# LSTM with residual on one core: the first PSUM banks begin without the bias, x and Wx load first, and step 4's plain products move into the first h Wh

## The chip, the cores and the metric

The kernel runs on one core of one Trainium2 chip. The metric is the device time of one execution in microseconds; the median of several runs is compared. A core has TensorE (PE) for matmuls, which write to eight PSUM banks of 128 x 512 float32, VectorE (DVE), ScalarE (ACT), GpSimd (POOL), and SyncE (SP), which here issues the transfers. All arithmetic is float32.

## The reference

An LSTM over 512 steps for a batch of 32, input and hidden size 512, with a residual:

```
xW = x @ Wx + b                        # x (32, 512, 512), Wx (512, 2048)
for t in range(512):
    a = xW[:, t] + h @ Wh              # Wh (512, 2048), h starts as cond_1024, c as 0
    i, f, o = sigmoid(a[:, :512]), sigmoid(a[:, 512:1024]), sigmoid(a[:, 1024:1536])
    g = tanh(a[:, 1536:])
    c = f * c + i * g
    h = o * tanh(c)
    out[:, t] = x[:, t] + h
```

Only `h @ Wh` and what follows it depend on the step before. `x @ Wx` does not, and the kernel works it out ahead.

## The kernel before

One step's gates fill one PSUM bank of 128 x 512: the four column groups j of 32 partitions hold the batch of 32 for a quarter of the hidden units, and the free dimension holds four gates of 128. `h_part(t)` (L459) adds `h @ Wh` into it: for each of four row blocks k of Wh, four matmuls (one for each j) of 128 x 512. The profile counts each float32 matmul as two records, so a step has 32 of them. `cell(t)` (L472) applies sigmoid and tanh on ScalarE (L476 to L478), the products on VectorE (fc, ig, c, h at L485 to L493) and the transpose into `ht` (L495), which is the next step's stationary operand.

`x @ Wx` is done in two ways. From step 8 on (quads of four steps from `FIRST` = 2) it uses a fast matrix product of seven sub-products at two levels: sums of x blocks (`early_sums`, `late_sums`) and sums of weight blocks (`outer_weight` at L212, `inner_weight` at L217) are made on VectorE, multiplied in `inner` (L335) into the banks pa, pb and pp, and gathered by `first_add`, `second_add` and `seed` (L292 to L311). Steps 0 to 7 and the last eight use plain products instead: `direct(t, pairs)` (L355) adds the product of step t's x with pieces of Wx; a pair (k, gg) is one quarter of Wx, with two pieces e, and costs eight matmuls. Four pairs are the whole product of a step.

The banks of the steps are `ge` (even steps), `go[0]` (steps 1, 5, ...) and `go[1]` (steps 3, 7, ...). `clear(bank)` (L246) writes zeros with a matmul, after which products accumulate onto what is there. The bias gets into a step by being copied into the bank before the products (`set_bias`, on ScalarE, L379), or, at the very start, by the VectorE copies of L586. Step 2 has no bank of its own at the start; its products are made in step 3's bank, copied by ScalarE to SBUF (`park`, L387), and brought back later by `set_bias`.

The order on each engine is that in which the program is written (`tc.manual_schedule()`, L580). The main loop goes over k from 8 on, and k is called an iteration here: iteration k runs `h_part(k - 11)` if there is one, then the evacuations of the fast product (`evacuate`), bias copies, x sums, weight sums (`make_weights`, from the table `weights` at L515), the plain products of the start (`first_direct`, L544), the fast product's matmuls (`input_part`), the plain products of the table `direct_at`, and the cell. Iterations 8 to 10 have no step yet; iteration 11 has step 0.

Loads at the start (L194 to L208): half of x's chunk 0, two quarters of Wx, chunk 1 of x, two more quarters of Wx, four pieces of Wh and the other half of chunk 0 are issued by SP; the four bias pieces, each broadcast to 32 partitions, and h0 by ScalarE's queue. Transfers share eight semaphores in turn, so an issue may have to wait until the transfer eight places earlier has landed. In the trace x chunks are `xc`, the quarters of Wx `w`, the pieces of Wh `wh_sb`.

`start_sums` (L259) prepares db, a difference of bias parts, and the running sums xr1 and xr5 from the bias. In VectorE's order it stands between the first two weight sums and the first outer one.

Of the kernel before, what the change touches and what calls it, by code (L numbers as in the profile page):

```python
# [7 lines left out]
F32 = mybir.dt.float32  # L8
# [3 lines left out]
P = 128  # L12
# [16 lines left out]
def kernel(  # L29
# [38 lines left out]
    nc = tc.nc  # L68
# [4 lines left out]
    upool = ctx.enter_context(tc.tile_pool(name="upool", bufs=1))  # L73
# [9 lines left out]
    pp = psum.tile([P, 4, P], F32, name="pp")  # L83
    ge = psum.tile([P, G, P], F32, name="ge")
    go = [psum.tile([P, G, P], F32, name=f"go_{i}") for i in range(2)]
# [3 lines left out]
    def gates_of(t):  # L89
        if t >= 4 * LAST:  # L90
            return last_banks[t - 4 * LAST]
        return ge if t % 2 == 0 else go[(t % 4) // 2]
# [80 lines left out]
    def load_first(half):  # L173
        n = TC // 2
        nc.sync.dma_start(
            out=xcs[0][:, half * n : (half + 1) * n].rearrange("p t q b -> p (t q b)"),
            in_=x[0][:, half * n * P : (half + 1) * n * P],
        )

    bias_sb = const.tile([P, G, P], F32, name="bias_sb")  # L180
    h_init = const.tile([P, NJ, B], F32, name="h_init")
# [5 lines left out]
    def load_raw(k, gg):  # L187
        for e in range(2):
            nc.sync.dma_start(
                out=raw[k, gg][:, 2 * e : 2 * e + 2].rearrange("p s j u -> p (s j u)"),  # L190
                in_=wx[2 * k + gg][:, 2 * e * NJ * P : 2 * (e + 1) * NJ * P],
            )

    load_first(0)  # L194
    for j in range(NJ):
        nc.scalar.dma_start(
            out=bias_sb[j * B : (j + 1) * B, :, :],
            in_=bias[j].unsqueeze(0).to_broadcast([B, G, P]),
        )
    nc.scalar.dma_start(out=h_init.rearrange("p q b -> p (q b)"), in_=h0)  # L200
    load_raw(0, 0)
    load_raw(0, 1)
    load_chunk(1)
    load_raw(1, 0)
    load_raw(1, 1)
    for k in range(NJ):
        nc.sync.dma_start(out=wh_sb[:, k], in_=wh[:, k])
    load_first(1)  # L208

    def outer_weight(r):  # L210
        a, b = {5: (w12, w_sb[1]), 7: (w_sb[3], w12), 6: (w_sb[3], w_sb[5]), 4: (w_sb[2], w_sb[6])}[r]
# [143 lines left out]
    def direct(t, pairs, bank=None):  # L355

        c, tt = divmod(t, TC)
        bank = gates_of(t) if bank is None else bank
        fresh = not written(bank)
        for k, gg in pairs:  # L360
            for e in range(2):
                for j in range(NJ):
                    nc.tensor.matmul(  # L363
                        bank[j * B : (j + 1) * B, 2 * gg : 2 * gg + 2],
                        xcs[c][:, tt, 2 * k + e],
                        raw_blocks(k, gg, e, t >= 4 * LAST)[:, :, j],
                        start=fresh and (k, gg, e) == (0, 0, 0),
                        stop=True,
                        skip_group_check=True,
                    )  # L370

    def written(bank):

        return bank in (ge, *go, pp)

    parked = {}

    def set_bias(t):
        nc.scalar.copy(gates_of(t), parked.pop(t, bias_sb))  # L379

    def add_bias(t):
        nc.vector.tensor_add(gates_of(t), gates_of(t), bias_sb)

    def park(t, bank):

        parked[t] = upool.tile([P, 4, P], F32, name="parked", tag="u3")
        nc.scalar.copy(parked[t], bank)  # L387

    def quad_at(r, k, stage):

# [3 lines left out]
    def evacuate(k):  # L394

        for r in (1, 5, 6, 7):
            q = quad_at(r, k, 4)
            if q is not None:
                read_out(r, q)
        for q, rest in (divmod(k - 7, 4),):  # L400
            if rest == 0 and FIRST <= q < LAST:
                nc.vector.tensor_add(U[23, q][:, 1], U[7, q], U["p5", q])
        for q, rest in (divmod(k - 10, 4),):
            if rest == 0 and FIRST <= q < LAST:
                nc.vector.tensor_add(U["p5", q], U[4, q], U["p5", q])  # L405
        for q, rest in (divmod(k - 12, 4),):
            if rest == 0 and FIRST <= q < LAST:
                p5 = U["p5", q]
                nc.scalar.copy(ge[:, 2:4], p5[:, 0:2])
                nc.scalar.copy(go[1][:, 2:4], p5[:, 2:4])  # L410
        q = quad_at(2, k, 1)
        if q is not None:
            first_add23(q)
        for r in (5, 1, 4, 6, 7):
            q = quad_at(r, k, 1)
            if q is not None:
                first_add(r, q)
        q = quad_at(2, k, 2)
        if q is not None:
            second_add23(q)  # L420
        for r in (6, 7, 5, 4, 1):
            q = quad_at(r, k, 2)
            if q is not None:
                second_add(r, q)
        q = quad_at(2, k, 3)
        if q is not None:
            seed23(q)
        for r in (4, 6, 7, 5, 1):
            q = quad_at(r, k, 3)
            if q is not None:  # L430
                seed(r, q)
# [27 lines left out]
    def h_part(t):  # L459
        g = gates_of(t)  # L460
        for k in range(NJ):
            for j in range(NJ):
                nc.tensor.matmul(  # L463
                    g[j * B : (j + 1) * B],
                    state["ht"][:, k, :],
                    wh_sb[:, k, j, :],
                    start=False,
                    stop=True,
                    skip_group_check=True,
                )  # L470

    def cell(t):  # L472
# [44 lines left out]
        0: [(1, 7), (5, 6)],  # L517
        1: [(1, 4), (5, 7), 6, (6, 5)],
        2: [(5, 4), (6, 6)],
        3: [(6, 7), (2, 5), (3, 5)],  # L520
        4: [4, (6, 4)],
        5: [7, (7, 5)],
        6: [(7, 6), (2, 6), (3, 6), (4, 5)],
        7: [(7, 7), (2, 7), (3, 7)],
        8: [(7, 4), (4, 6)],
        9: [(3, 4)],
        10: [(2, 4), (4, 7)],
# [6 lines left out]
    def make_weights(k):  # L534
        for what in weights.get(k - 4 * FIRST, ()):
            make(what)


    ALL = ((0, 0), (0, 1), (1, 0), (1, 1))
    bias_at = {12: (2,), 13: (5,), 14: (4,), 15: (7,), 16: (6,)}  # L540
    direct_at = {k: [(t, ALL) for t in bias_at[k] if t > 2] for k in bias_at}
    direct_at[11], direct_at[12] = [(3, ALL[2:3])], [(3, ALL[3:4])]

    def first_direct(k):  # L544

        pairs = {8: ALL[0:2], 9: ALL[2:3], 10: ALL[3:4]}.get(k, ())
        for pair in pairs:
            direct(2, (pair,), gates_of(3))
            if k == 10:
                park(2, gates_of(3))  # L550
                set_bias(3)
            for t in (0, 1):
                direct(t, (pair,))
        if k == 10:
            direct(3, ALL[0:2])

# [4 lines left out]
    for k in range(504, WINDOWS):  # L561
# [9 lines left out]
        while todo and free_at[todo[0][0] - end] <= k and room > 0:  # L571
            t = todo[0][0]
# [7 lines left out]
    with tc.manual_schedule():  # L580
        warm = work.tile([P, G, P], F32, name="warm", tag="s")
        nc.scalar.activation(warm[:, 0], zero, AF.Sigmoid)
        for bank in (go[1], ge, go[0], pp):
            clear(bank)
        for t in (3, 0):
            nc.vector.tensor_copy(gates_of(t), bias_sb)  # L586
        set_bias(1)
        for what in weights[-1][:2]:
            make(what)
        start_sums()  # L590
        make(weights[-1][2])
        for op in early_sums(nc.vector, 1):
            op()
        make(weights[-1][3])
        early, late = {}, {}
        for k in range(4 * FIRST, WINDOWS):
            t = k - LEAD
            c, rest = divmod(k + 5, TC)
            if rest == 0 and 2 <= c < NCHUNK:
                load_chunk(c)  # L600
            if k == 4 * LAST + 1:
                reload()
            if t >= 0:
                h_part(t)
            evacuate(k)
            for i in bias_at.get(k, ()):
                set_bias(i)
            for i in bias_after:
                if bias_after[i] == k:
                    add_bias(i)  # L610
            for first, sums_of, made, cut in ((-1, early_sums, early, 5), (3, late_sums, late, 3)):
                c, rest = divmod(k - first, TC)
                if (2 if sums_of is early_sums else 1) <= c < NCHUNK - 1 and rest in (0, 2):
                    if rest == 0:
                        made[c] = sums_of(nc.vector, c)
                    for op in made[c][:cut] if rest == 0 else made.pop(c)[cut:]:
                        op()
            make_weights(k)
            if t < 0:
                first_direct(k)  # L620
            input_part(k)
            if t >= 0:
                for what in direct_at.get(k, ()):
                    direct(*what)
                cell(t)
# [43 lines left out]
```

## Time and profile before

| | us |
|---|---|
| median of 3 runs (lowest to highest) | 3164.57 (3163.84 to 3165.09) |
| the profiled execution | 3164.18 |
| its span, first to last instruction | 3162.3 |
| TensorE busy in the span | 3148.0 |
| VectorE busy | 2234.3 |
| ScalarE busy | 1274.1 |
| first plain product starts | 9.33 |
| h Wh of step 0 starts, its last piece starts | 24.88, 28.84 |
| h Wh of steps 1, 2, 3, 4, 5 starts | 31.99, 37.87, 45.63, 54.04, 63.33 |

When the inputs landed in the profiled execution, worked out as issue plus time to landing: first half of x 3.9 us; bias pieces 3.7, 5.4, 7.4, 8.45; h0 8.6; Wx pieces 6.3, 8.2, 9.9, 11.2, then 13.6, 14.9, 17.6, 18.9; chunk 1 of x 12.35; Wh pieces 21.3, 23.8, 26.3, 28.8; second half of x 29.4.

Times are of one execution by the profiler; what lies outside the span is 1.9 us. Matmuls are pipelined and overlap in the records, so lengths of groups are best read from start to start. A row of the timeline gives start, duration, engine, line, operation, destination and sources, shape and count, and in brackets the idle time of the engine before it and what ended it.

### The profile page before, as it was taken

What the parts mean: (1) busy time and instruction counts of PE and PEld (TensorE: products, weight loads), DVE (VectorE), ACT (ScalarE), POOL (GpSimd) and SP (SyncE); (2) the same over time, 40 slices, a digit from 0 to 9 for tenths busy, and PEclk for the clock granted to TensorE, in tenths of its full rate; (3) what the DMA queues carried; (4) which work ended last, traced back from release to release, by engine and by line L of the source; (5) the groups of instructions that cost most, each with busy time, mean ns of one, the idle gap of its engine ahead of it and who ended that gap; (6) DMA issues with size and microseconds to landing.
All of it is one profiled execution on the core that took longest, in us unless ns stands there. A gap on an engine that the chain in (4) does not pass through costs nothing.

```text
span 3162.3 us, 149307 instructions
## 1 busy us (share of the span) xinstructions
PE 3148.0 (100%) x66048; PEld 1894.6 (60%) x66048; DVE 2234.3 (71%) x9242; ACT 1274.1 (40%) x4186; POOL 237.5 (8%) x515
## 2 busy tenths in 40 slices
PE   9999999999999999999999999999999999999999
PEld 5666666666666666666666666666666666666653
DVE  6777777777777777777777777777777777777763
ACT  2434444444444444444344444444444444443432
POOL 0000000000000000000000000000000000000000
PEclk9999999999999999999999999999999999999999
DMA  3000000000000000000000000000000000000010
GB/s 137 26 28 20 28 20 28 26 21 26 27 21 28 20 28 26 20 28 20 28 27 21 26 28 20 28 20 28 26 21 26 22 25 27 21 26 28 20 34 13
DMA packets 49370, 86.45 MB, mean 27 GB/s; under 512 B 5456, under 2 KB 38480, under 8 KB 48208
## 3 DMA queue, kind: packets, MB, share of 16 engines
q1 hardware_dynamic: 48384, 76.57, 7.4%
q8 instruction: 516, 8.45, 1.1%
q14 instruction: 134, 1.10, 0.1%
q10 hardware_dynamic: 336, 0.33, 0.0%
HBM read 43.32 MB, written 33.55 MB: 24 GB/s over the span
## 4 chain that ended last, share of the span: by engine, by line
PE 98%; DMA 1%; DVE 1%; ACT 0%; issue 0%; ACTq 0%; DVEq 0%
PE ge L463 27%; PE go L463 27%; PE pa L335 18%; PE pp L335 10%; PE pb L335 6%; PE ge L335 5%; PE go L335 3%; DMA wh_sb<-in_L_cond_Wh_dram 1%; PE go L363 0%; PE pa L463 0%; PE ge L363 0%; PE pa L363 0%; DMA xc<-in_x_dram 0%; DMA bias_sb<-in_L_cond_b_dram 0%; PE pp L463 0%; PE pb L463 0%
## 5 line engine op out<-in xcount | busy, mean ns | idle before, releaser
L463 PE MATMUL go<-wh_sb,ht 128*32 128x512 f32 x8128 | 918.7, 592 | 0.0
L463 PE MATMUL ge<-wh_sb,ht 128*32 128x512 f32 x8064 | 911.5, 592 | 0.7 <-DVE ht L495 0.5
L485 DVE TENSOR_TENSOR fc<-s,c 128x128 f32<-128x128 f32 x511 | 149.3, 292 | 569.1 <-ACT s L476 569.1
L463 PEld LDWEIGHTS go<-wh_sb,ht 128*32 128x32 f32 x8128 | 256.7, 110 | 458.0 <-issue 455.1
L463 PEld LDWEIGHTS ge<-wh_sb,ht 128*32 128x32 f32 x8064 | 256.9, 110 | 455.4 <-issue 415.7
L506 POOL TENSOR_TENSOR oc<-xc,ht 128x128 f32<-128x128 f32 x511 | 237.3, 464 | 2915.9 <-DVE ht L495 1466.4
L476 ACT ACTIVATE s<-ge 128x256 f32<-128x256 f32 x253 | 97.2, 384 | 833.8 <-PE ge L463 833.8
L335 PE MATMUL pa<-w,n 128*32 128x128 f32 x5952 | 299.1, 273 | 1.4 <-DVE xr L296 1.4
L491 ACT ACTIVATE ig<-c 128x64 f32<-128x64 f32 x1024 | 205.8, 248 | 220.9 <-DVE c L489 220.9
L476 ACT ACTIVATE s<-go 128x256 f32<-128x256 f32 x254 | 97.5, 384 | 441.7 <-PE go L463 441.7
L493 DVE TENSOR_TENSOR fc<-s,ig 128x64 f32<-128x64 f32 x1024 | 189.9, 226 | 96.7 <-ACT ig L491 96.7
L335 PEld LDWEIGHTS pa<-w,n 128*32 128x32 f32 x5952 | 180.7, 110 | 78.8 <-issue 39.1
L335 PEld LDWEIGHTS pa<-w,na 128*32 128x32 f32 x3968 | 124.1, 110 | 148.8 <-issue 110.8
L275 ACT COPY u<-pp 128x512 f32<-128x512 f32 x248 | 145.4, 586 | 142.0 <-PE pp L335 142.0
L335 PE MATMUL pp<-w,sa 128*32 128x128 f32 x3968 | 199.4, 273 | 0.0
L335 PE MATMUL pa<-w,na 128*32 128x128 f32 x3968 | 199.4, 273 | 0.0
L335 PE MATMUL pa<-w,nb 128*32 128x128 f32 x3968 | 199.4, 273 | 0.0
L495 DVE STREAM_TRANSPOSE ht<-fc 128x64 f32<-128x64 f32 x1024 | 190.6, 224 | 1.5 <-DVE fc L493 0.9
L487 DVE TENSOR_TENSOR ig<-s 128x64 f32<-128x64 f32 x1024 | 181.1, 219 | 0.0
L489 DVE TENSOR_TENSOR c<-fc,ig 128x64 f32<-128x64 f32 x1024 | 180.5, 217 | 0.0
L405 DVE TENSOR_TENSOR p<-u,p 128x512 f32<-128x512 f32 x124 | 86.0, 694 | 114.5 <-ACT u L275 114.5
L335 PEld LDWEIGHTS pa<-w,nb 128*32 128x32 f32 x3968 | 121.4, 110 | 74.1 <-issue 37.9
(138 smaller groups left out, 5278.8 us busy)
## 6 DMA issues: line engine op xcount, KB each, us to landing
out_dram<-oc SPq DMA_DIRECT2D x255, 128.0 KB, 1.8
xc<-in_x_dram SPq DMA_DIRECT2D x63, 512.0 KB, 3.8
w<-in_L_cond_Wx_dram SPq DMA_DIRECT2D x10, 512.0 KB, 6.8
wh_sb<-in_L_cond_Wh_dram SPq DMA_DIRECT2D x4, 1024.0 KB, 14.6
xc<-in_x_dram SPq DMA_DIRECT2D x2, 256.0 KB, 9.5
bias_sb<-in_L_cond_b_dram ACTq DMA_DIRECT2D x4, 64.0 KB, 5.0
h_init<-in_cond_dram ACTq DMA_DIRECT2D x1, 64.0 KB, 6.0
out_dram<-oc SPq DMA_DIRECT2D x1, 64.0 KB, 1.6
```

The source lines that it names most:

```text
L275: nc.scalar.copy(u, pp)
L335: nc.tensor.matmul(dst[j * B : (j + 1) * B], operand(r, s, quad), w_sb[r][:, place(r, s), j], start=start, stop=True, skip_group_check=True,)
L405: nc.vector.tensor_add(U["p5", q], U[4, q], U["p5", q])
L463: nc.tensor.matmul(g[j * B : (j + 1) * B], state["ht"][:, k, :], wh_sb[:, k, j, :], start=False, stop=True, skip_group_check=True,)
L476: nc.scalar.activation(s[:, 0:2, :], g[:, 0:2, :], AF.Sigmoid)
L485: nc.vector.tensor_mul(fc, s[:, 1, :], state["c"])
L487: nc.vector.tensor_mul(ig[:, u], s[:, 0, u], s[:, 3, u])
L489: nc.vector.tensor_add(c[:, u], fc[:, u], ig[:, u])
L491: nc.scalar.activation(tc_t[:, u], c[:, u], AF.Tanh)
L493: nc.vector.tensor_mul(h[:, u], s[:, 2, u], tc_t[:, u])
L495: nc.vector.transpose(ht[:, 2 * i : 2 * i + 2].rearrange("p q b -> p (q b)"), h[:, u])
L506: nc.gpsimd.tensor_add(state["oc"][:, tt % 2], xcs[n][:, tt], ht)
```

## The change

- Loads: both quarters of Wx for k = 0 go ahead of the bias; the bias and h0 are issued by SP too, h0 after the other quarters of Wx; the second half of x's chunk 0 goes between Wh pieces 1 and 2.
- Banks: `clear(go[1])`, the two bias copies of L586 and `set_bias(1)` at the start go. For steps below 4 outside pp the first product starts the bank afresh (`fresh`). The bias of steps 0, 1 and 2 is added by VectorE after their products: step 2's as it is parked (a sum from bank to SBUF in place of ScalarE's copy), steps 0 and 1 by `add_bias` in iteration 10, step 3 by `add_bias` in iteration 13.
- Step 4: its plain products (four pairs, 64 records) leave iteration 14. They are made in the bank pp, which ScalarE fills with the bias at the start, between the Wh pieces of step 0: two pairs ahead of piece 2 and two ahead of piece 3. ScalarE then copies pp to SBUF (`parking(4, "u2")`), and `set_bias(4)` brings it back in iteration 14.
- Weight sums (2,5) and (3,5) move from iteration 11 to 14, (4,5) from 14 to 15. `make_weights` comes after `first_direct`.

The resulting order on VectorE at the end of iteration 10 and in 11 is: evacuations, the parking sum, add_bias(0), add_bias(1), two weight sums (L217), second_add(5), the lower half of seed(1) into pp (L311), three x sums, one weight sum, cell 0.

```diff
     load_first(0)
+    load_raw(0, 0)
+    load_raw(0, 1)
     for j in range(NJ):
-        nc.scalar.dma_start(
+        nc.sync.dma_start(
             out=bias_sb[j * B : (j + 1) * B, :, :],
             in_=bias[j].unsqueeze(0).to_broadcast([B, G, P]),
         )
-    nc.scalar.dma_start(out=h_init.rearrange("p q b -> p (q b)"), in_=h0)
-    load_raw(0, 0)
-    load_raw(0, 1)
     load_chunk(1)
     load_raw(1, 0)
     load_raw(1, 1)
+    nc.sync.dma_start(out=h_init.rearrange("p q b -> p (q b)"), in_=h0)
     for k in range(NJ):
+        if k == 2:
+            load_first(1)
         nc.sync.dma_start(out=wh_sb[:, k], in_=wh[:, k])
-    load_first(1)
...
-        fresh = not written(bank)
+        fresh = t < 4 and bank is not pp or not written(bank)
...
-    def park(t, bank):
-
-        parked[t] = upool.tile([P, 4, P], F32, name="parked", tag="u3")
-        nc.scalar.copy(parked[t], bank)
+    def parking(t, tag):
+
+        parked[t] = upool.tile([P, 4, P], F32, name=f"parked_{t}", tag=tag)
+        return parked[t]
...
         for k in range(NJ):
+            if t == 0 and k >= 2:
+                direct(4, ALL[2 * k - 4 : 2 * k - 2], pp)
...
-        3: [(6, 7), (2, 5), (3, 5)],
+        3: [(6, 7)],
...
-        6: [(7, 6), (2, 6), (3, 6), (4, 5)],
-        7: [(7, 7), (2, 7), (3, 7)],
+        6: [(7, 6), (2, 5), (3, 5), (2, 6), (3, 6)],
+        7: [(7, 7), (2, 7), (3, 7), (4, 5)],
...
-    direct_at = {k: [(t, ALL) for t in bias_at[k] if t > 2] for k in bias_at}
+    direct_at = {k: [(t, ALL) for t in bias_at[k] if t not in (2, 4)] for k in bias_at}
...
             if k == 10:
-                park(2, gates_of(3))
-                set_bias(3)
+                nc.vector.tensor_add(parking(2, "u3"), gates_of(3), bias_sb)
             for t in (0, 1):
                 direct(t, (pair,))
+                if k == 10:
+                    add_bias(t)
...
-        for bank in (go[1], ge, go[0], pp):
+        for bank in (ge, go[0], pp):
             clear(bank)
-        for t in (3, 0):
-            nc.vector.tensor_copy(gates_of(t), bias_sb)
-        set_bias(1)
+        nc.scalar.copy(pp, bias_sb)
...
                 h_part(t)
+            if t == 0:
+                nc.scalar.copy(parking(4, "u2"), pp)
             evacuate(k)
...
-            make_weights(k)
+            if k == 13:
+                add_bias(3)
             if t < 0:
                 first_direct(k)
+            make_weights(k)
             input_part(k)
```

## The prediction, made before the changed kernel was run

> **What bounds the kernel now.** I read the page's busy shares first, then the busy times by stretch, then TensorE's waits in the first 140 us, then the timeline of 8 to 38 us, engine by engine. Shares of the whole run:
>
> ```profile
> PE 3148.0 (100%) x66048; PEld 1894.6 (60%) x66048; DVE 2234.3 (71%) x9242; ACT 1274.1 (40%) x4186; POOL 237.5 (8%) x515
> ```
>
> By stretch (us, then busy time of TensorE, its weight loads, VectorE, ScalarE, GpSimd, clock, DMA share, GB/s):
>
> ```profile
> 5.40:9.30 3.90, 1.02 (x12) 0.12 (x4) 0.72 (x2) 0.59 (x1) 0.00 (x0) 1.00 1.04 377
> 9.30:14.50 5.20, 5.17 (x96) 3.15 (x100) 5.08 (x8) 0.00 (x0) 0.00 (x0) 1.00 1.04 411
> 14.50:19.20 4.70, 3.36 (x68) 1.81 (x60) 4.56 (x16) 0.00 (x0) 0.00 (x0) 1.00 1.02 415
> 19.20:24.40 5.20, 5.17 (x104) 3.15 (x104) 5.17 (x9) 1.18 (x2) 0.00 (x0) 1.00 1.03 424
> 24.40:28.80 4.40, 3.23 (x42) 1.11 (x40) 4.37 (x10) 0.38 (x1) 0.00 (x0) 1.00 0.88 355
> 54.00:3162.30 3108.30, 3100.79 (x65271) 1869.46 (x65260) 2193.40 (x9131) 1260.80 (x4149) 235.01 (x507) 1.00 0.08 24
> ```
>
> After 54 us TensorE is the bound (3100.8 of 3108.3 us). Every edit lies before it, so the result is the old time plus the shift of the moment at which the unchanged stream resumes. From 9.3 to 28.8 us VectorE is as full as TensorE or fuller (19.18 against 16.93 of 19.5 us), and that is the lead to follow. TensorE's waits up to 140 us:
>
> ```profile
> PE go L363 <- DVE go L586: 2.9, 1, 2.9
> PE pa L335 <- DVE xr L296: 1.4, 1, 1.4
> PE ge L463 <- DMA wh_sb<-in_L_cond_Wh_dram: 1.2, 1, 1.2
> ```
>
> The change aims at the first and the third; the second is VectorE's. Its order, from the timeline:
>
> ```profile
> 8.58 0.69 DVE L586 COPY go<-bias_sb 128x512 f32<-128x512 f32 x1 [7.44 <-DMA bias_sb<-in_L_cond_b_dram]
> 9.77 1.41 DVE L217 TENSOR_TENSOR w<-w 128x512 f32<-128x512 f32 x2
> 11.10 0.42 DVE L260 TENSOR_TENSOR db<-bias_sb 128x256 f32<-128x256 f32 x1
> 12.37 2.29 DVE L212 TENSOR_TENSOR w<-w,w 128x2048 f32<-128x2048 f32 x1
> 14.57 0.22 DVE L109 TENSOR_TENSOR n<-xc 128x64 f32<-128x64 f32 x1
> 18.90 0.28 DVE L296 TENSOR_TENSOR xr<-pa,bias_sb 128x128 f32<-128x128 f32 x1
> ```
>
> From 8.58 us to 27.0 VectorE never stops. It begins when the bias lands, and the changed order still has db (L260), a reader of the bias, ahead of L212 and L109.
>
> **The skill.** The Trainium skill, PSUM — Partial Sum Buffer, section on bank collisions, says two engines must not touch one bank and quadrant at once, and to guard by bank, not by address. The trace agrees: VectorE's L311 (lower half of pp) stood 0.27 us for ScalarE's L310 (upper half). DMA: Bandwidth & Descriptors, section Queues, rings and completion order, says the SP and ACT issues have a ring each on the same 16 engines, which take turns between rings and start descriptors of one ring in order. The trace agrees that they interleave: bias pieces landed 3.0 to 6.3 us after issue beside the first Wx piece, which took 5.1. Moved to SP's ring, the bias stands behind x and four Wx pieces.
>
> **Part by part.** B is the time at which the bias has landed.
>
> *Loads.* Before it, B was 8.45 (last piece issued at 2.15 us, 6.3 to land). Now 2304 KB (x half 256, four Wx pieces of 512) go first, and it closes 2560 KB. Lower end: all of it at 410 GB/s, the settled rate, from 2.0 us is 8.4, with 0.4 for completion 8.8. Upper end: in the old run the second w12 piece closed almost the same set of bytes (2624 KB, with bias and h0) and landed at 11.2 us, so 11.0. The old run had slow slices between 3 and 8 us, with bias rows in between and few transfers issued (the third Wx piece waited until 3.9 us for a free semaphore; now the first seven or eight issue at once). I take B = 10.1. The first Wx piece should land near 5 us (was 6.3), its second near 6.5 (was 8.2).
>
> *First products.* They no longer wait for L586 at 9.27: clears are three instead of four (1.7 + 1.6 + 0.85 from 1.2, so until 5.4), and the first product starts near 5.4 instead of 9.33, 3.9 us earlier. But products of banks (0,0) and (0,1) cost 16 matmul records, 0.87 us, per bank and pair; three banks and two pairs are 5.2 us, done near 11.4, and then pb<-w,n needs n (L109).
>
> *VectorE's chain from B.* The two copies at L586 (0.6 each) are gone from its head; the two L217 products (1.33) now run while it waits for the bias. Start to start in the old trace: db to L212 1.27, L212 to n 2.20, n to L296 4.33, L296 to the next L296 (L297, two L217, L212, L217) 4.65, then 0.73 for three evacuations. So n starts at B+3.47, L296 at B+7.80, the parking sum at B+13.18, done at B+13.87. The three added 128x512 sums (parking, two add_bias) cost 0.69 each, taken from L327, the same size with a PSUM operand, 0.62 start to start.
>
> *TensorE follows it.* Pause before pb until B+3.7, then 0.22 and 2.6 for pair (1,0). Pause before pa until B+8.1 (L296 plus the 0.33 seen). Then 0.68 and 2.6, ending at B+11.4. Then direct(3) writes bank go1, which the parking sum still reads: a new pause until B+13.9, 2.5 us. In the old kernel ScalarE did that parking at 21.03 us and TensorE did not stop. Then direct(3) 1.73, two pa groups 0.43, Wh pieces 0 and 1 1.72, step 4's first half 1.73, piece 2 0.86, second half 1.73: B+22.1 = 32.2 us; piece 3 then ends at 33.1. Wh piece 3 landed at 28.8 us and the second x half, now ahead of two Wh pieces, adds 0.6; it is not late, so the third wait vanishes under this work.
>
> *What stands behind pp.* ScalarE can copy pp to parked_4 only after B+22.1: 0.27 for the drain (as at L476 after L463), 0.59, then L310 0.38 and gaps: B+23.4. VectorE's L311 waits for it by the bank rule, and being in order holds up its next work: L311 to the last inner sum 1.32, one L217 0.62, only then fc of cell 0: B+25.34. ScalarE's gates would have been ready about 1.6 us sooner. From fc to the first h Wh product of step 1 the old trace has 30.39 to 31.99, 1.60: B+26.94. At B = 10.1 that is 37.0 against 31.99, +5.0.
>
> *What is given back.* Iteration 14 loses its 64 records of step 4 (3.45 us at 50.6). From h Wh of step 3 to that of step 4 the old trace has 45.63 to 54.04, 8.41. Now TensorE has 3.43 + 7 x 0.22 = 4.97, but cell 3 takes 2.29 after the last product (29.70 to 31.99 in cell 0), so 5.72: 2.69 back, and 0.75 of the removed work turns into a wait. add_bias(3) (0.62) goes into iteration 13, where ht was ready at 44.6 and wanted at 45.63: hidden by 3.45 us of step 5's products, with 0.4 us to spare; without that cover it costs its 0.62. The weight products moved to iterations 14 and 15 (0.62 each) fit: VectorE idled 1.66 and 1.88 us there, and iteration 15 has 9.3 us of TensorE work over it.
>
> Sum: B + 26.94 - 31.99 - 2.69 = B - 7.74. At 10.1 it is +2.4 us. The profiled execution took 3164.18 with a span of 3162.3; so 3164.7 of span and 3166.5 in all; the median of the runs is 0.4 higher, hence 3167.0. A shift under 6.3 us (0.2%) is about what this measurement can't tell from no change.
>
> **Rivals.**
> (1) *The early start is kept.* If VectorE's chain didn't decide, the 3.9 us gained at the first product would survive: 3160.7. For it: TensorE's own work from 5.4 us could fill the time. Against: n, L296 and the parking sum stand in VectorE's fixed order behind the bias.
> (2) *The bias lands early.* If its small pieces are served as fast as the quickest in the old run (3.0 us from an issue near 4.0), B = 7.0 and the sum is -0.7: 3163.8. It turns to a gain below B = 7.74. Against: it would have to pass 2 MB queued on its ring.
> (3) *The clock drops* (slower by more than 0.2%). TensorE: Matmul & The Clock Gate, part 1, says the clock halves after an idle window of about 3.4 us and takes as long to return. New pauses of about 2, 1.6 and 2.5 us come within 12 us. The cold clears took 1.7 us where warm ones took 0.85, so a drop costs up to 1.7; with 2.4 already lost it takes three drops to pass 6.3: 3167.0 + 5.1 = 3172.1. Against: 2.9 us of idle before 9.33 did not slow the next products.
> (4) *The start isn't moved at all*, if w lands no sooner than 9.3: then B is over 10.5 as well, and the sum is +2.8 or more, up to +3.3 at 11.0: 3167.9. It differs little from my forecast.
>
> **How the numbers follow.** Forecast (B from 8.8 to 11.0, with 0.8 for the sums): 0.78, own range 3164.9 to 3168.7. Case 4: 0.08. Case 1: 0.06, case 2: 0.05, case 3: 0.03. To leave no more than 2 in 10 out, with 0.7 us between runs and single clock drops of up to 1.7 us above: 3163.8 to 3169.6. Only case 3 passes 0.2% above; only case 1, with more waits gone than I can see, could pass it below (6.3 us of the roughly 8 us that TensorE waited in all from 5.4 us on): faster 0.02, slower 0.03, same 0.95.
>
> **What would show it.** Right: first product near 5.4 us; VectorE idle until db at 9 to 11; TensorE waiting for n, for xr (L296's successor) and about 2.5 us for the parking sum; VectorE standing some 6 us at the lower pp sum until ScalarE's copies; h Wh of step 1 at 36 to 38 us; a TensorE pause of about 0.8 us before h Wh of step 4. Wrong: a chain of waits in which DMA of Wh or of the second x half ends one, matmuls of doubled duration after 12 us, no stop at the parking sum, or h Wh of step 4 before 54 us.

## The result, and the profile after

| | before | after |
|---|---|---|
| median of 13 runs each, us | 3163.99 | 3171.05 |
| lowest to highest | 3163.77 to 3165.09 | 3168.98 to 3172.59 |
| the profiled execution | 3164.18 | 3169.08 |
| its span | 3162.3 | 3167.3 |

The changed kernel takes 7.06 us more: a ratio of 1.0021, 95% interval 1.0013 to 1.0030. Its runs also scatter more, over 3.6 us instead of 1.3. The profiled execution lies at the lower edge of that scatter; how far that can be explained is part of what follows.

The busy shares and the long stretch of the changed kernel answer to those of before. First the page's busy times:

```profile
PE 3148.4 (99%) x66040; PEld 1893.7 (60%) x66040; DVE 2236.4 (71%) x9244; ACT 1273.5 (40%) x4185; POOL 237.5 (7%) x515
```

Then the busy times by stretch (TensorE, weight loads, VectorE, ScalarE, GpSimd, clock, DMA share, GB/s):

```profile
5.40:11.15 5.75, 3.78 (x64) 1.69 (x56) 1.28 (x2) 0.00 (x0) 0.00 (x0) 1.00 1.03 314
11.15:16.00 4.85, 2.64 (x52) 1.52 (x56) 3.68 (x7) 0.59 (x1) 0.00 (x0) 1.00 1.02 396
54.00:3167.30 3113.30, 3104.97 (x65344) 1871.53 (x65336) 2201.13 (x9153) 1263.50 (x4157) 235.95 (x508) 1.00 0.08 24
```

TensorE is still full after 54 us; as before, only the start decides. There it begins earlier (5.8 us, was 9.33), but has only 3.78 of 5.75 us of work, and then 2.64 of 4.85: VectorE worked 1.28 us in the first of these stretches. TensorE's waits up to 140 us in the changed kernel:

```profile
PE go L364 <- DVE parked L553: 2.3, 1, 2.3
PE go L364 <- DMA w<-in_L_cond_Wx_dram: 2.1, 2, 1.3
PE pb L336 <- DVE n L109: 2.1, 1, 2.1
PE pa L336 <- DVE xr L297: 1.4, 1, 1.4
PE go L466 <- DVE ht L498: 1.3, 1, 1.3
...
PE ge L466 <- DVE ht L498: 0.7, 1, 0.7
```

The wait of 2.9 us for L586 and the one of 1.2 us for the last piece of Wh are gone. In their place stand the parking sum (2.3), the block sum n (2.1), Wx (2.1), and two waits for ht (1.3 in step 1, 0.7 in step 4). All of these but the Wx wait lead back to VectorE. Its timeline in the changed kernel:

```profile
12.19 0.42 DVE L261 TENSOR_TENSOR db<-bias_sb 128x256 f32<-128x256 f32 x1 [4.29 <-DMA bias_sb<-in_L_cond_b_dram]
...
13.47 2.28 DVE L213 TENSOR_TENSOR w<-w,w 128x2048 f32<-128x2048 f32 x1
15.67 0.22 DVE L109 TENSOR_TENSOR n<-xc 128x64 f32<-128x64 f32 x1
...
19.99 0.28 DVE L297 TENSOR_TENSOR xr<-pa,bias_sb 128x128 f32<-128x128 f32 x1
...
25.38 0.68 DVE L553 TENSOR_TENSOR parked<-go,bias_sb 128x512 f32<-128x512 f32 x1
...
35.66 0.43 DVE L312 TENSOR_TENSOR pp<-pa,xr 128x256 f32<-128x256 f32 x1 [6.82 <-ACT pp L311]
...
37.60 0.28 DVE L488 TENSOR_TENSOR fc<-s,c_init 128x128 f32<-128x128 f32 x1
```

VectorE stands idle for 4.29 us until the bias has landed, at 12.19 us; in the kernel before it had the bias at 8.45. Later it stands for 6.82 us until ScalarE is done with pp. How these join is seen in the chain that ended last, here its part from 5 to 36 us (start, length, what):

```profile
5.07 7.10 DMA bias_sb<-in_L_cond_b_dram
...
26.12 1.93 PE go L364 x32
...
30.20 1.73 PE pp L364 x32
31.93 0.86 PE ge L466 x8
32.79 1.77 PE pp L364 x32
34.64 0.59 ACT parked L608
35.26 0.39 ACT pp L311
35.66 0.43 DVE pp L312
```

The chain begins with the fourth bias piece, 7.1 us from issue to landing, runs along VectorE to the parking sum, goes over to TensorE, which is from there on full but with step 4's products in its row, and comes back to VectorE through ScalarE's copies of pp. From there h Wh of steps 1 to 5 starts at 39.19, 45.08, 52.83, 58.75 and 68.04 us (31.99, 37.87, 45.63, 54.04, 63.33 before): 7.2 us late in step 1, 4.7 late in steps 4 and 5. At the end of the span it is 5.0; the last 0.3 is lost in small steps later on.

### The profile page after: what moved, and what is told of

It reads as the page before. It is cut to its first block, busy times and chain, and to the rows that moved or that the text cites. A ratio compares the mean times of both kernels' runs of the same rounds, so it can differ in the third digit from the quotient of the medians.

```text
span 3167.3 us, 149297 instructions
## 1 busy us (share of the span) xinstructions
PE 3148.4 (99%) x66040; PEld 1893.7 (60%) x66040; DVE 2236.4 (71%) x9244; ACT 1273.5 (40%) x4185; POOL 237.5 (7%) x515
## 3 DMA queue, kind: packets, MB, share of 16 engines
q8 instruction: 516, 8.45, 1.1%
## 4 chain that ended last, share of the span: by engine, by line
PE 98%; DVE 1%; ACT 0%; DMA 0%; SPq 0%; issue 0%; DVEq 0%; ACTq 0%
PE ge L466 27%; PE go L466 27%; PE pa L336 18%; PE pp L336 10%; PE pb L336 6%; PE ge L336 5%; PE go L336 3%; PE go L364 0%; PE pa L466 0%; PE pa L364 0%; DMA bias_sb<-in_L_cond_b_dram 0%; PE pp L364 0%; DVE w L213 0%; PE ge L364 0%; DVE w L218 0%
```

## The experiments

Each experiment carries its run's name in brackets; the tables further down use it. B is, as in the prediction, the time at which the bias has landed. A drop is a stretch in which TensorE's granted clock was below 1.00. Medians of before beside them were 3164.11 us in the first session (again, filler, bias_act, step4_back), 3164.04 in the second (bias_first, no_bias, loads_only, best) and 3163.99 in the third (best_warm, banks_only).

**The changed kernel once more (again).** No edit; the question is whether its scatter goes with the landing of the bias or with the clock.

> The changed kernel once more, for a second profile. Theory A (the late bias alone): a span of 3167 to 3168 us with every stretch of the first 60 us at full clock; runs differ because the bias lands at different times, so the time at which db (L261) starts should account for the difference to the first profile, us for us. Theory B (the new pauses also let the clock drop): at a span of 3168.5 us or more, one or two stretches of some 3.4 us after 12 us at about half clock, with db within 1 us of 12.2.

It took 3170.95 us, with a span of 3169.2. VectorE's first work on the bias, from the timeline of this run:

```profile
14.04 0.42 DVE L261 TENSOR_TENSOR db<-bias_sb 128x256 f32<-128x256 f32 x1 [3.91 <-DMA bias_sb<-in_L_cond_b_dram]
```

By stretch, the clock is the figure after GpSimd's:

```profile
9.00:12.00 3.00, 2.62 (x28) 1.37 (x32) 0.69 (x1) 0.00 (x0) 0.00 (x0) 0.58 1.03 309
```

The bias landed 1.85 us later than in the first profile and the span is 1.9 us longer, as theory A has it. A's full clock was not seen, though: it was 0.58 in the stretch from 9 to 12 us, where it had been 1.00, and 0.85 from 12 to 15 us, in all 1.7 us of clock. This cost nothing to speak of: TensorE's wait for n behind it became shorter, 1.6 instead of 2.1 us. The Trainium skill, TensorE: Matmul & The Clock Gate, Part 1, says that the window which measures activity runs freely and that the same kernel can therefore meet it differently. Two profiles of one kernel, with 1.00 and 0.58, fit this but don't decide it, because TensorE had also waited longer for a Wx piece in the second (2.3 us against 0.8).

**TensorE kept busy in its pauses (filler).**

```diff
         for pair in pairs:
             direct(2, (pair,), gates_of(3))
+            if pair == (0, 1):
+                clear(pa[2])
...
+        for _ in range({8: 2, 9: 1, 10: 2}.get(k, 0)):
+            clear(pa[2])
```

> Zero products into bank pa[2], which nothing uses yet, fill the pauses of TensorE in iterations 8 to 10 (six clears of 8 records, 0.86 us each). They add at most 0.3 us to the path. Theory A: nothing changes but these 0.3 us; median 3171.0 to 3171.5 and the same spread of 3.6 us between runs. Theory B: TensorE stays busy, the clock stays full in all runs, median 3168.8 to 3169.6 and a spread near that of the kernel before, 1.3 us.

3170.55 us (3169.74 to 3171.53, 14 runs), ratio 1.0020, interval 1.0013 to 1.0028. The landing of the bias and the stretch from 9 to 12 us in its profile:

```profile
13.78 0.43 DVE L261 TENSOR_TENSOR db<-bias_sb 128x256 f32<-128x256 f32 x1 [4.01 <-DMA bias_sb<-in_L_cond_b_dram]
```

```profile
9.00:12.00 3.00, 2.97 (x32) 1.47 (x36) 0.69 (x1) 0.00 (x0) 0.00 (x0) 0.53 1.07 291
```

From 12 us on the clock was 1.00, and the span was 3168.9. The median lies between what the two theories named (A 3171.0 to 3171.5, B 3168.8 to 3169.6), and the spread of 1.8 us is nearer to B's 1.3 than to A's 3.6, so the times alone don't decide between them. The profiles do, for the drops that they hold: the span less B is 3155.1 us here, with a drop to 0.53 and none after 12 us, 3155.1 in the first profile with no drop, and 3155.2 in again. A drop before the landing cost nothing here; the landing of the bias counted in full.

What the executions without a kept profile did stays open in part. Three of the changed kernel's 13 have a mean clock that rounds to 1.000, and they are its three fastest (3168.98 to 3169.63 us); the other ten have 0.998 or 0.999. Late transfers and drops came together in the profiles of again and filler, where TensorE had stood idle for Wx, so this doesn't contradict the reading; but a drop behind the parking sum, where TensorE is full, isn't ruled out for them.

**The bias on ScalarE's queue again, issued first (bias_act).** The rest of the change stays.

```diff
     load_first(0)
-    load_raw(0, 0)
-    load_raw(0, 1)
     for j in range(NJ):
-        nc.sync.dma_start(
+        nc.scalar.dma_start(
             out=bias_sb[j * B : (j + 1) * B, :, :],
             in_=bias[j].unsqueeze(0).to_broadcast([B, G, P]),
         )
+    load_raw(0, 0)
+    load_raw(0, 1)
```

> The four bias pieces go back to ScalarE's ring, ahead of Wx; everything else stays changed. The bias should land near 8.5 us; the first outer weight sum (L213) then waits for the second w12 piece at 11.2 us, which is as good as a bias at 10.0. Against the profile's 12.2 that is 2.2 us off the start of every later step: span 3165.1 us in a run at full clock, 3166.9 in all. Theory A: median 2.2 below the changed kernel's 3171.05, so 3168.8. Theory B: the pause ahead of pb shrinks from 2.1 us to under 0.5, fewer drops, median 3166.9 to 3168.

3168.22 us (3166.4 to 3169.61, 21 runs), ratio 1.0012, interval 1.0005 to 1.0018; span of the profile 3165.4. VectorE's timeline shows that another transfer now sets the pace:

```profile
9.56 0.42 DVE L261 TENSOR_TENSOR db<-bias_sb 128x256 f32<-128x256 f32 x1
...
11.54 2.29 DVE L213 TENSOR_TENSOR w<-w,w 128x2048 f32<-128x2048 f32 x1 [0.62 <-DMA w<-in_L_cond_Wx_dram]
```

The bias is no longer waited for (db starts right behind the weight sums), but L213 needs the second quarter of Wx, which lands at 11.5 us. That is the start that B = 10.27 would give. Below this the bias can't help. The median lies between the two theories' figures, 3168.8 for A and at most 3168 for B; the span is the 3165.1 worked out for A, and 0.3 more.

**Step 4's products back in iteration 14 (step4_back).**

```diff
-            if t == 0 and k >= 2:
-                direct(4, ALL[2 * k - 4 : 2 * k - 2], pp)
...
-    direct_at = {k: [(t, ALL) for t in bias_at[k] if t not in (2, 4)] for k in bias_at}
+    direct_at = {k: [(t, ALL) for t in bias_at[k] if t > 2] for k in bias_at}
...
-        nc.scalar.copy(pp, bias_sb)
...
-            if t == 0:
-                nc.scalar.copy(parking(4, "u2"), pp)
```

> Step 4's products return to iteration 14 and pp isn't used for them; loads and bias as changed. If the copies behind pp hold up cell 0 as worked out, h Wh of step 1 comes at B+21.8 instead of B+27.0 (34.0 us at B = 12.2) and 2.7 us are not given back: about 2.5 us less than the changed kernel, median 3168.5, full-clock span 3164.8. If the moved products fill time that is lost anyway, it is slower by up to 2.7 us: 3171 to 3173.7. VectorE should not stand at the lower pp sum.

3168.92 us (3166.86 to 3170.73, 19 runs), ratio 1.0015, interval 1.0008 to 1.0022. VectorE's timeline:

```profile
30.90 0.42 DVE L312 TENSOR_TENSOR pp<-pa,xr 128x256 f32<-128x256 f32 x1
...
34.92 0.29 DVE L486 TENSOR_TENSOR fc<-s,c_init 128x128 f32<-128x128 f32 x1 [2.01 <-ACT s L477]
```

The bias landed at 12.97 us. The stop of 6.82 us at L312 is gone, and fc waits for ScalarE's gates instead. By stretch:

```profile
27.00:33.00 6.00, 6.00 (x72) 2.96 (x76) 4.42 (x10) 0.00 (x0) 0.00 (x0) 0.72 0.48 199
```

In this execution the clock fell twice, to 0.72 here and also from 15 to 21 us. h Wh of step 1 began at 36.53 us, 1.7 us later than B + 21.8 = 34.8; in the stretch shown TensorE was full, and 6.0 us at 0.72 lose 1.7. Without the stop at pp TensorE is the bound there, and a drop counts. In the medians step 4's edit costs 3171.05 - 3168.92 = 2.1 us: what it takes from iteration 14 is less than what it puts in front of cell 0. In the profiles the span less B is 3154.1, and without the 1.7 of the drop 3152.4, against 3155.1 with the edit, so at full clock it costs 2.7.

**The bias first on SP's queue (bias_first), and no bias at all (no_bias).** The first moves the four bias pieces ahead of x and Wx; the second does not load the bias.

```diff
+    for j in range(NJ):
+        nc.sync.dma_start(
+            out=bias_sb[j * B : (j + 1) * B, :, :],
+            in_=bias[j].unsqueeze(0).to_broadcast([B, G, P]),
+        )
     load_first(0)
     load_raw(0, 0)
     load_raw(0, 1)
-    for j in range(NJ):
-        nc.sync.dma_start(
-            out=bias_sb[j * B : (j + 1) * B, :, :],
-            in_=bias[j].unsqueeze(0).to_broadcast([B, G, P]),
-        )
```

> The four bias pieces stay on SP's ring but go ahead of x and Wx; all else as changed. It tells two readings of the late bias apart. Theory P (its place behind 2.3 MB decides): the bias is there by 5 us and no longer counts; VectorE's chain then starts at the second w12 piece. Theory Q (bias pieces waiting in the ring also slow the Wx pieces ahead of them, which moved at 250 to 390 GB/s until the bias had landed): with the bias gone by 5 us, Wx moves at 400 GB/s from there and that piece lands near 9.5 us, L213 at 9.8, span 3155.1 + 8.5 = 3163.6, median 3165.3. Theory R (transfers are slow in the first 9 to 13 us whatever is in them): it lands at 11.5 to 13, span 3165.5 to 3167, median 3167 to 3168.5.

```diff
-    for j in range(NJ):
-        nc.sync.dma_start(
-            out=bias_sb[j * B : (j + 1) * B, :, :],
-            in_=bias[j].unsqueeze(0).to_broadcast([B, G, P]),
-        )
+    nc.gpsimd.memset(bias_sb, 0.0)
```

> The bias isn't loaded at all: bias_sb is zeroed by GpSimd, so the bias is left out of the computation. All else as changed. Theory Q: the second w12 piece lands by 9 us, L213 near 9.2, span near 3163, median 3164.8. Theory R: it lands near 11.3 us as in the changed kernel, L213 at 11.5, span 3165.3, median 3167.

bias_first: 3169.46 us (3167.8 to 3170.36, 20 runs), 1.0017 (1.0010 to 1.0023). no_bias: 3167.70 us (3166.36 to 3170.31, 20 runs), 1.0012 (1.0005 to 1.0019). VectorE's first outer weight sum, in bias_first and then in no_bias:

```profile
13.31 2.29 DVE L213 TENSOR_TENSOR w<-w,w 128x2048 f32<-128x2048 f32 x1 [0.53 <-DMA w<-in_L_cond_Wx_dram]
```

```profile
11.27 2.29 DVE L209 TENSOR_TENSOR w<-w,w 128x2048 f32<-128x2048 f32 x1 [1.07 <-DMA w<-in_L_cond_Wx_dram]
```

In bias_first the bias was there by about 4 us, but the last piece of the second Wx quarter landed at 13.3, a little later than any of the theories had it, and L213 began at 13.31, which answers to B = 12.0; the span was 3167.1. In no_bias the Wx piece landed at 11.2, as in the changed kernel (11.25), n began at 13.48, and the span was 3165.5, close to theory R. So ahead of Wx the bias delays Wx, behind Wx it is itself late, and without any bias the chain still can't begin before Wx is there: in both the slow first transfers are the limit. The runs of no_bias scatter over 4.0 us without a bias to wait for, so the landing of the bias isn't all that scatters.

**The loads alone, on the kernel before (loads_only).**

```diff
     load_first(0)
+    load_raw(0, 0)
+    load_raw(0, 1)
     for j in range(NJ):
-        nc.scalar.dma_start(
+        nc.sync.dma_start(
...
+    nc.sync.dma_start(out=h_init.rearrange("p q b -> p (q b)"), in_=h0)
     for k in range(NJ):
+        if k == 2:
+            load_first(1)
         nc.sync.dma_start(out=wh_sb[:, k], in_=wh[:, k])
-    load_first(1)
```

> The kernel before with the new load order alone. The bias lands at 12 to 14 us; VectorE then has the two early copies (1.2) ahead of db, but the two L217 products come behind them too: L212 at B+3.9 as before (8.45 to 12.37). Wh is not late by then. Every start to h Wh of step 1 moves by B - 8.45 less the 1.65 us that TensorE waited for Wh: span 3162.3 + 2 to 4, median 3166 to 3168. If the load order helped, as a start of products at 5 us would, it would be below 3164.

3168.05 us (3167.16 to 3169.28, 20 runs), 1.0013 (1.0006 to 1.0019). TensorE's waits:

```profile
PE go L364 <- DVE go L587: 8.4, 1, 8.4
```

The bias landed at 14.3 us; the wait for it, 2.9 us in the kernel before, became 8.4. The wait for the last Wh piece is gone here too, but by the lateness of all else. On the kernel before the load order alone costs 3168.05 - 3164.04 = 4.0 us.

**The banks alone (banks_only).** Old loads, step 4 in iteration 14; the banks of steps 0 to 3 begin without the bias and VectorE adds it. The weight sums stay where the change put them. The cut shows the main parts, against the kernel before.

```diff
-        fresh = not written(bank)
+        fresh = t < 4 and bank is not pp or not written(bank)
...
-                park(2, gates_of(3))
-                set_bias(3)
+                nc.vector.tensor_add(parking(2, "u3"), gates_of(3), bias_sb)
...
+                if k == 10:
+                    add_bias(t)
...
-        for t in (3, 0):
-            nc.vector.tensor_copy(gates_of(t), bias_sb)
-        set_bias(1)
```

> The change without its loads and without its step 4 edit: only the banks begin without the bias and VectorE adds it later. Theory A (the time is set by VectorE's chain from the bias, and the chain by when the bias and the first Wx quarter land): with the old loads the first outer sum starts near 11.5 us as in the run with the bias on ScalarE's ring, which answers to B of 10.3; without the wait at pp, h Wh of step 1 is at B + 21.8 = 32.1 us against 31.99 before, nothing is given back in iteration 14, so median 3164.2 us, no change; a clock drop on TensorE's way can add up to 1.7 us (3165.9). Theory P (the parking sum and the two sums with the bias cost more than the chain of B shows): h Wh of step 1 is 2 us or more behind 31.99 at a full clock, and the median 3166 us or more.

3165.30 us (3164.1 to 3166.47, 13 runs), 1.0004 (0.9996 to 1.0012). TensorE's waits:

```profile
PE go L363 <- DVE parked L550: 2.3, 1, 2.3
PE go L363 <- DMA w<-in_L_cond_Wx_dram: 2.2, 2, 1.7
```

h Wh of step 1 began at 32.26 us (32.1 expected by A, 31.99 before), at a full clock, with a span of 3162.9. The wait of 2.9 us for the bias copies is away, and nothing is won: 2.2 us go to Wx and 2.3 to the parking sum. VectorE's L212 began at 11.66 us here, which answers to B = 10.39; h Wh of step 1 is then at B + 21.9 (21.8 worked out), and the span at B + 3152.5. So the chain through the loads holds. The median is 1.1 us above A's figure, within what A left for a drop (3165.9); whether it is a drop or a later landing of Wx in the other executions this run can't say.

In a row, the medians give each part its price: banks (with the moved weight sums) 3165.30 - 3163.99 = 1.3 us, then the loads 3168.92 - 3165.30 = 3.6, then step 4 3171.05 - 3168.92 = 2.1; in all 7.1. The first of these can't be told from nothing (interval 0.9996 to 1.0012). With the bias on ScalarE's queue step 4 costs 3168.22 - 3165.30 = 2.9, though that kernel differs from banks_only in the places of h0 and of x's second half too.

**A version put together from this (best).** The kernel before, with: ScalarE copying the bias into the banks of steps 3, 0, 1 and pp, instead of VectorE; the first outer weight sum in two halves; the weight sums (1,7) and (5,6) an iteration later; x of steps 0 to 4 in the first x piece; and step 4's products in pp at the end of iteration 10, ahead of h Wh of step 0 instead of inside it.

```diff
...
-        0: [(1, 7), (5, 6)],
-        1: [(1, 4), (5, 7), 6, (6, 5)],
+        1: [(1, 7), (5, 6), (1, 4), (5, 7), 6, (6, 5)],
...
         if k == 10:
             direct(3, ALL[0:2])
+            direct(4, ALL, pp)
+            parked[4] = upool.tile([P, 4, P], F32, name="parked_4", tag="u2")
+            nc.scalar.copy(parked[4], pp)
...
-        for t in (3, 0):
-            nc.vector.tensor_copy(gates_of(t), bias_sb)
-        set_bias(1)
+        for t in (3, 0, 1):
+            set_bias(t)
+        nc.scalar.copy(pp, bias_sb)
```

> The kernel before with what the runs point to: bias on ScalarE's ring as before; the early bias copies all on ScalarE (VectorE loses 1.2 us of work ahead of db); the first outer weight sum in two halves, so that its first half needs no second w12 piece; weight sums (1,7) and (5,6) behind first_add of iteration 9; steps 0 to 4 in the first piece of x; step 4's products in pp ahead of the first h Wh piece, so that ScalarE's copy of pp runs under h Wh and VectorE doesn't stand at the lower pp sum. Then TensorE waits for the last Wx piece (19 us) and is full from there; h Wh of step 0 ends 0.7 us later than before, and 2.7 us come back in iteration 14: 2.0 us faster, median 3162.1. If the early products or copies cost more than seen, 3163 to 3165.

3164.33 us (3163.79 to 3165.81, 13 runs), ratio 1.0001, interval 0.9993 to 1.0009: no change from before, where 3162.1 had been expected. TensorE's timeline has its first products late, and the second group of sixteen at 1.90 us instead of about 1.05:

```profile
9.94 1.08 PE L364 MATMUL go<-w,xc 128*32 128x256 f32 x16 [3.72 <-ACT go L380]
10.83 1.90 PE L364 MATMUL ge<-w,xc 128*32 128x256 f32 x16
```

By stretch:

```profile
9.00:12.00 3.00, 2.06 (x28) 1.13 (x32) 2.79 (x6) 2.15 (x4) 0.00 (x0) 0.81 1.02 407
12.00:15.00 3.00, 3.00 (x40) 1.59 (x36) 2.90 (x9) 0.00 (x0) 0.00 (x0) 0.62 1.03 410
```

After 3.72 us of idle the clock fell, on a path that now is TensorE's. The next run (best_warm) takes only that away.

```diff
-        for bank in (go[1], ge, go[0], pp):
+        for bank in (go[1], ge, go[0], pp, pa[2], pa[2], pa[2], pa[2]):
             clear(bank)
```

> The version before this one (profile span 3162.6 us, median 3164.33) lost about 1.7 us between 9 and 15 us, where the granted clock was 0.81 and then 0.62 after TensorE had stood idle from 6.2 to 9.9 us for the bias. Here four more clears of an unused bank (about 0.85 us each, 3.4 us) fill that pause; all else is the same. Theory C (the pause lowers the clock and the lower clock is on the path): clock 1.0 from 9 to 15 us, h Wh of step 1 near 32.7 us instead of 34.42, span near 3160.9, median near 3162.6 us. Theory N (the clears don't hold the clock, or VectorE decides anyway): h Wh of step 1 stays near 34.4 us and the median near 3164.3 us.

3163.40 us (3163.03 to 3163.76, 13 runs), ratio 0.9998, interval 0.9990 to 1.0006. TensorE's timeline and the busy times by stretch:

```profile
6.79 3.61 PE L250 MATMUL pa<-zero 128*32 128x512 f32 x32
...
11.09 1.04 PE L364 MATMUL ge<-w,xc 128*32 128x256 f32 x16
```

```profile
9.00:12.00 3.00, 3.00 (x52) 1.33 (x48) 2.58 (x6) 2.15 (x4) 0.00 (x0) 1.00 1.03 410
12.00:15.00 3.00, 3.00 (x64) 1.70 (x60) 2.93 (x8) 0.00 (x0) 0.00 (x0) 1.00 1.03 407
```

The four added clears fill the pause, and the clock stays at 1.00. From the first product (10.23 us) to h Wh of step 1 it is now 33.48 - 10.23 = 23.25 us, against 34.42 - 9.94 = 24.48: the drop had cost 1.2 us, less than the 1.7 expected. The span, 3161.6, is 1.0 shorter, so theory C holds in kind. All 13 runs of best_warm, each with a mean clock that rounds to 1.000, are faster than all 13 of best, each with 0.999. The median is 0.6 us below that of before and 7.65 below the changed kernel's; the 0.6 is inside the interval.

## Why the prediction was wrong

The time lies outside its range, 1.45 us above the upper end and 4.05 above the number. The mechanism was right and one term, B, was mis-sized.

**The step that failed: "Loads".** It took B = 10.1, between 8.8 and 11.0. Measured: 12.19, 14.04 and 13.78 us in three profiles in which the order of loads and of VectorE's work is the changed kernel's, 12.97 and 14.3 in two that share its loads. Every profile with the rest of the change then lies on one line (B of the three in brackets is read from VectorE's stream: start of L213 less 1.27):

| profile | B | span | span - B |
|---|---|---|---|
| after | 12.19 | 3167.3 | 3155.1 |
| again | 14.04 | 3169.2 | 3155.2 |
| filler | 13.78 | 3168.9 | 3155.1 |
| bias_act | (10.27) | 3165.4 | 3155.1 |
| bias_first | (12.04) | 3167.1 | 3155.1 |
| no_bias | (10.0) | 3165.5 | 3155.5 |

So the span follows B one for one, in profiles with no drop and in profiles with one or two before 15 us. The median of 3171.05, less the 1.8 outside the span of the profiled execution (3169.08 - 3167.3), is a span of about 3169.3 and so a B near 14.2. B varied by 1.85 us between two profiles, so the greater scatter of the runs may go the same way; for the executions without a kept profile both are inferences, and drops or the landing of Wx may have a part in them. From 3167.0 to 3171.05 it is then 4.1 us for B, 0.5 for the rest of the span, and 0.5 back for what was added outside it: the prediction took the median as 0.4 above the profiled execution from three runs, and in 13 runs it is 0.2 below.

Three parts of the step can be sized from the packets in the traces, since the bias moves in rows of 2 KB and Wx in rows of 4 KB. The step's lower end had the 2304 KB ahead of the bias through at 7.8 us, the bias itself in 0.6 more, and 0.4 for completion. Measured, in the first profile and in again:

- the first row of the bias moved at 9.2 us in both, 1.4 later than that;
- its last row was through at 11.3 and 12.9 us, so 256 KB took 2.1 and 3.8 us instead of 0.6;
- it was reported as landed 0.9 and 1.1 us after that; the 0.4 had no source.

The middle part is the largest and the one that varies. The step counted the bytes up to the end of the bias, 2560 KB or 2.62 MB, as if they passed in order. By the mean rates of the trace this much had been moved by 10.2 us in the first profile and by 10.9 in that of again; but when the bias landed, 3.23 and 3.71 MB were through (265 and 264 GB/s over 12.19 and 14.04 us). Of these 0.6 and 1.1 MB of later transfers, 0.3 and 0.7 had moved before the last row of the bias, the rest between that row and the report. The Trainium skill has this: DMA: Bandwidth & Descriptors, section Two DMAs through the same engine are not ordered, says that nothing orders transfers across the 16 engines. The trace agrees: rows of the next transfer moved from 9.9 us on beside the bias's in the first profile, and the step's reading of one ring as a line was too simple. The old kernel had the same overhang, 0.5 MB when w12 landed, so the upper end of 11.0 had it in, but at the old rate. The pieces were also issued later, the last at 5.1 us in the first profile (2.15 before), when the bulk ahead of it was still moving; how much that adds no run shows.

The rate from 9 to 12 us was lower in every kernel whose bias goes through SP's ring (GB/s, by stretch; no packet of a load moves before 1.7 us):

| | 0 to 9 us | 9 to 12 us | 12 to 15 us |
|---|---|---|---|
| after | 243 | 325 | 414 |
| again | 223 | 309 | 394 |
| filler | 218 | 291 | 354 |
| step4_back | 244 | 262 | 395 |
| loads_only | 217 | 305 | 343 |
| bias_first | 194 | 328 | 422 |
| before | 254 | 408 | 410 |
| bias_act | 250 | 410 | 418 |
| banks_only | 241 | 403 | 423 |
| best | 230 | 407 | 410 |
| best_warm | 233 | 410 | 407 |
| no_bias (none loaded) | 242 | 408 | 423 |

Beside 262 to 328 with the bias on SP's ring stand 403 to 410 with it on ScalarE's or not loaded. The prediction had seen the slow slices of before between 3 and 8 us and taken it that they would pass at the same time; with the bias on SP's ring they lasted to 12 us and, in filler and loads_only, beyond. That it is the bias's rows that are slow isn't shown: in bias_first they had landed by about 4 us, and the rate from 9 to 12 us was 328 all the same. What slows this ring, and why the first 9 us are slow in all kernels, stays open.

**Rightly worked out.** VectorE's chain from B: n at B + 3.48 (3.47 predicted), L297 at B + 7.80 (7.80), the parking sum at B + 13.19 (13.18). TensorE follows it: the new pause at direct(3) is 2.33 us, until B + 13.9 (2.5, until B + 13.9), and Wh piece 3 starts at B + 22.1, without a wait for Wh. What stands behind pp: L312 at B + 23.5 (23.4), fc at B + 25.4 (25.34), h Wh of step 1 at B + 27.0 (26.94). What is given back: from step 3 to step 4 it is 5.92 us, 5.72 predicted, with the pause of 0.75 as it was named; 2.49 us come back, not 2.69. In all the span of the sum was 3154.6 + B, where 3155.1 + B was measured: 0.2 came back less, and 0.3 was lost after step 5, where the sum had nothing. Step 4's edit was worked out at 26.94 - 21.8 - 2.69 = +2.45 and costs 2.6 to 2.7 in the profiles at full clock (27.0 - 21.9 - 2.49), 2.1 in the medians (2.9 with the early bias). The stop at L312 has the predicted length, but only its last 0.4 us, ScalarE's upper half of pp, is the bank rule; the rest is the copy that has to read pp before it is written over. Of the signs named, two numbers missed, both through B: db started after 11 us, and h Wh of step 1 came after 38.

**The first products** began as predicted (5.8 us for 5.4), but were done near 13.7, not 11.4 (the sum's own terms, 5.4 and 5.2, give 10.6), as the second Wx quarter came at 11.25 us. This was hidden, because n came later still, at 15.67.

**The rivals.** (1) The early start was not kept: 3.5 us at the first product brought nothing. (2) was unlikely and is also wrong in itself: B below 7.74 would not have been a gain, because Wx at 11.2 to 11.5 us puts a floor of about 10.0 under the start of the chain (no_bias, bias_act). The sum lacked this second leg: with B at 10.0 at best it could not have come below +2.3 us. (3) named 3172.1 us, nearer to the median than the forecast, but for another reason: the clock did fall (0.58 in again), and while VectorE decides this is hidden; it costs 1.2 us (best) to 1.7 (step4_back) where TensorE is the bound. (4) did not happen: the products started at 5.8 us, and B was over 10.5 without it.

**The range.** It was set by B's bounds of 8.8 and 11.0. Both came from one execution of a kernel with another order of loads; 3 us more above, for a small transfer behind 2.3 MB, would have held the time and given the case of more than 0.2% far more than 0.03.

## What to carry to other kernels

Where one engine's stream in program order starts with a small input, ask first when that input lands, and put it on a queue of its own ahead of the bulk: here 256 KB behind 2.3 MB on one ring landed 3 to 6 us later than on a second ring (12.2 to 14.3 us for 8.45 and 8.9). An earlier start of the busiest engine is worth nothing while another engine's chain feeds it, and plain work put between the pieces of a critical product can cost more than its length: here 3.45 us of products cost 5.1, since they also held up VectorE's queue, and 2.5 came back later. When the last slack before a full TensorE is taken out, keep it busy through the remaining pause, since only then does a fallen clock count.

## What was not expected of the hardware

The same transfers moved at 262 to 328 GB/s from 9 to 12 us with the broadcast bias in SP's ring, and at 403 to 410 without it, with a DMA share of 0.95 to 1.07 in all of them: a full share says nothing of the rate. When a transfer landed, 0.5 to 1.1 MB issued after it had already been moved, and its report came 0.9 to 1.1 us after its last row (bias, two profiles). Four clears of an unused bank, 3.6 us of work with no use, held the clock at 1.00 and shortened the stretch after them by 1.2 us.
